# A four-layer conditioned network on one core: the layer-2 stencil with a turned result, row norms on ScalarE, and a planner with ranks by step

## The chip, the cores and the metric

The kernel runs on one core of a Trainium2 chip. The core has five engines with instruction queues of their own, each worked off in the order in which it was written: TensorE (PE; its weight loads are listed apart as PEld), VectorE (DVE), ScalarE (ACT), GpSimd (POOL) and SyncE (SP, which issues DMA transfers). They meet through semaphores. The metric is the device time of one launch in microseconds; the time before is 2741.08 us, the median of 3 runs (2740.74 to 2741.34).

## The reference, cut to what matters

Everything is fp32. A batch of 32 items, each a 256 x 256 matrix x (S tokens by D features), goes through four layers, one after the other:

```python
# layer 0: h from condB_t by two small linear layers; scale, shift = h @ Wsc + bsc, h @ Wsh + bsh
out = silu(scale * layer_norm(x) + shift) @ W_in + b_in        # norm over the whole 256x256 block
x = silu(scale * layer_norm(out) + shift) @ W_out + b_out + x
# layer 1: 16 heads of 16, 256 keys, a bias of 16x256x256 per item, padding mask
x = ln(x) * (1 + scale1) + shift1                               # norm over each row
x = x + softmax(q k^T / 4 + attention_bias, masked) v @ Wo
x = x + gelu_sigmoid(ln(x) * g2 + beta2 @ W1 + b1) @ W2 + b2
# layer 2: a finite-difference step on the 256x256 grid
Af, Bf = A_grid * f, B_grid * f
df = -(grad(Af[0], rows) + grad(Af[1], columns)) \
     + 0.5 * (grad2(Bf[0], rows) + grad2(Bf[1], columns) + mixed second derivative of Bf[2])
x = max(f + df * dt, 0)
# layer 3: causal attention with 16 heads and an exact-gelu feed-forward, gated by item
x = x + gate * (layer(x) - x)
```

`grad` and `grad2` are centred differences inside and one-sided ones in the first and last row or column. Along rows (partitions) they are a product with a banded 256 x 256 matrix.

## The kernel before, in words

A 256 x 256 matrix lies in SBUF as a tile [128, 2, 256]: row c*128 + p is on partition p. Weights stay in SBUF throughout. Each item runs through three generators, `layer_0`, `layer_1` (lines 931 and 956) and `layers_23` (line 1012), which record instructions and don't issue them.

The order is planned. `Order.record` notes each call with its engine, its dependencies, its length by a price list (`length`, line 145) and a rank, which is the value of `order.now` when it was recorded. The loop at lines 1087 to 1098 steps through all generators by time: item b's layer i starts at `b * PERIOD + START[i]`, and each `yield` moves its clock on by a nominal step times `PACE[i]`. `arrange` (line 186) then simulates the five engines and lets each take, of what is ready, the unit with the lowest rank; it counts PSUM banks (`CAPS`), a preference for staying in a tile shape on PE (`STAY`) and turns among the buffers of a tag. `emit` writes the instructions out in the order of their simulated starts. All instructions are therefore issued by line 327, and the profile has L327 for them; tiles tell them apart. So at one time PE works on layers of up to three items, in an order fixed when the kernel is built.

Steps that the text speaks of:

- The conditioning of layer 0 and layer 1 (lines 550 to 591), once: small matmuls with 128 x 128 weight blocks stationary and 32 items as moving columns; each block of the result gets its bias from one DVE instruction. Tiles `hidden`, `l0w`, `l0wss`, `w_ada`.
- `token_norm` (line 687): the norm of each row. DVE takes mean and variance, POOL the power -0.5 (`rstd`), and two DVE instructions write (x - mean) * rstd into tile `t`, which PE then turns (`mm<-ident,t`). Four calls an item: of x, of xm, of layer 2's x, of d.
- The stencil (lines 1024 to 1045). b2f, gd, a0f and b0f are products of f with grids; `gd` and `b0f` go through PE with the banded matrices `stencil` as stationary operand; `dd` (line 1052 on) is put together on DVE and added to the result. `small` holds products of edge columns.
- Attention: scores `sc` in four row groups of 32, bias subtracted by POOL (`nb`) and added by DVE with the running minimum (`pr`, `mn`), exponentials on ACT, transposes `tr` on PE, copied to `pt` by DVE and ACT in turns, and P·V in four column groups of 32.
- `add_row` and the differences on POOL write `x`, `xm`, `d`; all DMA transfers but a few at the start are issued by SP, in the planned order. Tile `x` has one buffer: the next item's load waits until this item's is read for the last time.

The lines of the stencil before:

```python
pm = mm_tile([P, C2, D])
for m in range(C2):
    with order.together():
        for i, u in enumerate((gd, b0)):
            for k in range(C2):
                pe.matmul(pm[:, m, :], lhsT=stencil[:, i, k, m * P : (m + 1) * P], rhs=u[:, k, :], ...)
```

Of the kernel before, what the change touches and what calls it, by code (L numbers as in the profile page):

```python
# [13 lines left out]
F32 = mybir.dt.float32  # L14
# [10 lines left out]
NFC = FF // P  # L25
HQ = 4
# [13 lines left out]
PERIOD = 90.3  # L40
START = (-51.7, 0.0, 118.1)
PACE = (1.27, 0.93, 1.0)
# [7 lines left out]
class Order:  # L50
# [8 lines left out]
    SETUP = 3e3  # L59
    HOP = 60.0  # L60
    TURN = 90.0
    SEEN = 165.0
    CAPS = {"sc": 5, "tr": 6, "mm": 8}
    EARLIER = {"sc": 12.4, "tr": -0.1, "mm": -2.0}
    STAY = 10.0
# [41 lines left out]
    def record(self, engine, call, method, args, kwargs):  # L107
# [11 lines left out]
        wide = [a for a in ins if math.prod(n for _, n in a.ap[1:]) >= 256]  # L119

        x["port"] = len(wide) > 1 and all(a.space != PSUM for a in ins + outs)
# [23 lines left out]
    def length(self, engine, method, outs, ins, args, kwargs):  # L145
# [5 lines left out]
        if engine == "pe":  # L151
# [5 lines left out]
            return max(free(outs[0]) / 1.2 + 2, 109.0) * passes, (rows, cols), slot  # L157
        if method == "dma_start":
            return sum(math.prod(k for _, k in a.ap) for a in outs) * 4
        if engine == "dve":  # L160
            if method == "reciprocal":
                return 120 + 8.3 * n, 40 + 8.3 * n
            if method == "tensor_tensor_reduce":
                return 240 + 1.05 * n, 150 + 1.05 * n
            if method == "tensor_scalar":
                a = (265 if columns else 150) + (1.06 if psum or not columns else 0.55) * n
            elif method == "scalar_tensor_tensor":
                a = 215 + 1.05 * n
            else:
                a = 148 + 1.05 * n  # L170
            return a, a - 80
# [8 lines left out]
        if method == "tensor_tensor":  # L180
            a = 600 if n <= 4 else 185 + 2.13 * n
        else:
            a = 185 + 0.86 * n
        return a, a - 40

    def arrange(self):
# [46 lines left out]
        dma = pool_end = 0.0  # L233
# [14 lines left out]
        while todo:  # L248
# [6 lines left out]
            for e in self.ENGINES:  # L255
                if free[e] > now:
                    continue
                while coming[e] and coming[e][0][0] <= now:
                    u = heapq.heappop(coming[e])[1]
                    heapq.heappush(ready[e][need[u]], (ranks[u], u))  # L260
                best = None
                for k, heap in ready[e].items():
                    if not heap or any(held[g] + m > room[g] for g, m in k):
                        continue
# [5 lines left out]
                    if best is None or rank < best[0]:  # L270
                        best = rank, k
# [8 lines left out]
                for x in units[u][2]:  # L280
                    if e == "pe":
# [4 lines left out]
                        elif its_shape != (P, P):  # L286
                            t = max(t, slots.get(slot, 0.0), pe_last + 6)
# [3 lines left out]
                        done = slots[slot] = t + one  # L291
                        pe_end = max(pe_end, done)
                        t = done if shape == (P, P) else t + 6
# [5 lines left out]
                    else:  # L299
                        x["start"] = now  # L300
                        more = 0.9 * max(pool_end - now, 0.0) if e == "dve" and x["port"] else 0.0
                        if e == "act" and x["length"][2] not in (None, table):
                            table, more = x["length"][2], self.TABLE
                        done, t = (now + a + more for a in x["length"][:2])
                        if e == "pool":
                            pool_end = done
                    end = max(end, done)
# [9 lines left out]
                for v in follow[u]:  # L317
                    may(v, now + 1)
                for v in after[u]:
                    may(v, now + 1 if units[v][0] == e and x["method"] != "dma_start" else end + self.HOP)  # L320

# [8 lines left out]
def _constants():  # L330
# [18 lines left out]
    stencil = np.stack([grad.T, grad2.T]).copy()  # L349
# [24 lines left out]
def kernel(ctx: ExitStack, tc: tile.TileContext, io, out, n_batch=B):  # L374
# [46 lines left out]
    scale_t = ctile("scale_t", [P, C2, B])  # L421
    shift_t = ctile("shift_t", [P, C2, B])
    ada_g = ctile("ada_g", [P, C2, B])
    ada_b = ctile("ada_b", [P, C2, B])
# [40 lines left out]
    def turned_vectors(tag, names, eng):  # L465
# [12 lines left out]
        return {name: cols[:, at] for name, at in vectors.items()}  # L478

    def load_x(b):  # L480
        x = sb.tile([P, C2, D], F32, tag="x", name="x", bufs=1)
# [7 lines left out]
    t_b = ctile("t_b", [P, B])  # L489
    sync.dma_start(t_b, io["condB_t"].partition_broadcast(P))  # L490
    vector = turned_vectors(
# [4 lines left out]
    i_b = ctile("i_b", [P, B], I32)  # L496
# [52 lines left out]


# [4 lines left out]
    pm = mm_tile([P, 4, B])  # L555
    for m in range(4):
        pe.matmul(pm[:, m, :], lhsT=w1[:, m * P : (m + 1) * P], rhs=enc, start=True, stop=True)
    for m in range(4):
# [575 lines left out]
```

## Time and profile before

| What | us |
| --- | --- |
| time, median of 3 runs | 2741.08 |
| profiled execution | 2742.87 |
| its span, first to last instruction | 2741.1 |
| PE busy | 2663.5 |
| DVE busy | 2327.2 |
| ACT busy | 1785.5 |
| POOL busy | 1537.2 |
| mean granted clock of PE, share of full | 0.993 |

The profile is of one execution. "Busy" is time in which at least one instruction of the engine ran. A line of groups reads: line, engine, operation, output<-inputs by tile names, shape and number, then busy us, mean ns of one, idle us ahead of them and who ended it. Matmuls are pipelined: an fp32 matmul shows as two instructions (passes) whose recorded durations overlap, so the pitch between starts tells what one costs. A line of stretches gives for each engine the busy time and (x number of instructions), then PE's granted clock, the busy share of DMA and its GB/s. A line of waits reads: who waited, for whom, total us, times, longest.

### The profile page before, as it was taken

The numbers are of one execution on the slowest core, as the hardware profiler recorded it, in microseconds if no ns is written. First come the engines' busy times: TensorE is split into PE (matmuls) and PEld (weight loads), VectorE is DVE, ScalarE is ACT, GpSimd is POOL, SyncE is SP. The second block draws the span as 40 slices with busy tenths as digits, with TensorE's granted clock in tenths as the row PEclk, the third lists the DMA queues.
The fourth block names the chain that finished last, engine by engine and source line by source line (L and its number), as shares of the span: only waits on it lengthen the run. The fifth ranks groups of instructions, "written<-read, shape, count | busy, mean of one in ns | idle before, by whom it ended". The sixth has DMA issues, their size and how long they took to land.

```text
span 2741.1 us, 59979 instructions
## 1 busy us (share of the span) xinstructions
PE 2663.5 (97%) x20330; PEld 2156.6 (79%) x20330; DVE 2327.2 (85%) x7665; ACT 1785.5 (65%) x5800; POOL 1537.2 (56%) x1896
## 2 busy tenths in 40 slices
PE   5899999999999999999999999999999999999997
PEld 5668888888888888888888888888888878888875
DVE  4689888889888888888888888888888888888873
ACT  1467676667677667667667667667667667667654
POOL 2556665556665556665556665556665556665430
PEclk9999999999999999999999999999999999999998
DMA  7222221112221112221112222112222112222100
GB/s 223 67 67 67 71 68 55 42 55 67 71 67 55 48 49 67 71 68 60 44 48 68 71 71 64 40 45 67 71 71 68 39 49 64 68 70 67 43 5 9
DMA packets 177446, 169.93 MB, mean 62 GB/s; under 512 B 19514, under 2 KB 175732, under 8 KB 177140
## 3 DMA queue, kind: packets, MB, share of 16 engines
q1 hardware_dynamic: 177104, 166.08, 19.7%
q8 instruction: 163, 2.67, 0.4%
q14 instruction: 143, 1.17, 0.1%
q10 hardware_dynamic: 36, 0.01, 0.0%
HBM read 157.66 MB, written 8.39 MB: 61 GB/s over the span
## 4 chain that ended last, share of the span: by engine, by line
PE 76%; POOL 13%; DVE 5%; DMA 2%; issue 2%; ACT 1%; SPq 0%; ACTq 0%; POOLq 0%; DVEq 0%
PE mm L327 60%; PE tr L327 10%; POOL nb L327 8%; PE sc L327 6%; POOL d L327 2%; DVE pr L327 1%; POOL rstd L327 1%; DVE st L327 1%; DVE d L327 1%; DMA nb<-in_fside_Bx16xSxS_dram 1%; POOL wide L327 1%; DVE t L327 1%; ACT pr L327 1%; DMA L1b<-in_L_cond_b_dram 0%; SPq L327 0%
## 5 line engine op out<-in xcount | busy, mean ns | idle before, releaser
L327 ACT ACTIVATE pr<-pr,mn 128x256 f32<-128x256 f32 (+1 forms) x2048 | 962.8, 477 | 218.7 <-DVE mn L327 214.2
L327 POOL TENSOR_TENSOR nb<-mask_f,nb 128x512 f32<-128x512 f32 x512 | 707.5, 1407 | 43.5 <-DMA nb<-in_fside_Bx16xSxS_dram 29.2
L327 PE MATMUL tr<-ident,pr 128*128 128x128 f32 x3584 | 507.4, 276 | 22.8 <-DVE mn L327 13.7
L327 PEld LDWEIGHTS tr<-ident,pr 128*128 128x128 f32 x3584 | 413.7, 141 | 119.2 <-ACT pr L327 50.3
L327 DVE CUSTOM_DVE_ANT_0 pr<-sc,nb 128x256 f32<-128x256 f32 x1024 | 379.7, 416 | 56.1 <-POOL nb L327 31.8
L327 ACT ACTIVATION_READ_ACCUMULATOR pr<-pr,mn 128x1 f32 x2048 | 396.7, 194 | 0.0
L327 DVE COPY pt<-tr 128x512 f32<-128x512 f32 (+1 forms) x512 | 308.4, 613 | 43.1 <-PE tr L327 42.8
L327 ACT COPY pt<-tr 128x512 f32<-128x512 f32 (+1 forms) x512 | 267.3, 528 | 104.5 <-PE tr L327 102.8
L327 DVE CUSTOM_DVE_ANT_0 pr<-sc,causal 128x128 f32<-128x128 f32 (+1 forms) x1024 | 296.1, 353 | 6.9 <-PE sc L327 6.8
L327 PE MATMUL sc<-k_t,nq 32*128 32x256 f32 (+1 forms) x4096 | 267.4, 374 | 0.0
L327 PE MATMUL mm<-h_t,L1w 128*128 128x256 f32 x1024 | 265.4, 390 | 0.6 <-DVE h_t L327 0.6
L327 PE MATMUL mm<-h_t,L3w 128*128 128x256 f32 x1024 | 247.0, 386 | 0.6 <-DVE h_t L327 0.6
L327 POOL TENSOR_SCALAR hid<-hid 128x256 f32<-128x256 f32 x256 | 124.9, 500 | 217.2 <-ACT hid L327 214.6
L327 PE MATMUL mm<-L3w,hid 128*128 128x256 f32 x1024 | 239.2, 382 | 4.3 <-ACT hid L327 4.3
L327 PE MATMUL mm<-L1w,hid 128*128 128x256 f32 x1024 | 240.0, 382 | 0.0
L327 PEld LDWEIGHTS mm<-L1w,hid 128*128 128x128 f32 x1024 | 187.1, 190 | 31.4 <-issue 9.9
L327 PEld LDWEIGHTS sc<-k_t,nq 32*128 32x128 f32 x4096 | 161.6, 184 | 62.8 <-issue 23.8
L327 PEld LDWEIGHTS mm<-L3w,hid 128*128 128x128 f32 x1024 | 189.3, 192 | 27.5 <-ACT hid L327 5.1
L327 PEld LDWEIGHTS mm<-h_t,L3w 128*128 128x128 f32 x1024 | 189.3, 192 | 27.0 <-DVE h_t L327 1.0
L327 ACT ACTIVATE k_t<-mm,cols 128x256 f32<-128x256 f32 x128 | 53.6, 470 | 233.0 <-PE mm L327 233.0
L327 PEld LDWEIGHTS mm<-h_t,L1w 128*128 128x128 f32 x1024 | 179.3, 192 | 26.8 <-DVE o L327 9.9
L327 POOL COPY wide<-rs 128x256 f32<-128x256 f32 x128 | 64.3, 502 | 192.4 <-DVE rs L327 179.7
(167 smaller groups left out, 4983.1 us busy)
## 6 DMA issues: line engine op xcount, KB each, us to landing
nb<-in_fside_Bx16xSxS_dram SPq DMA_DIRECT2D x512, 256.0 KB
x<-in_x_dram SPq DMA_DIRECT2D x32, 256.0 KB
out_dram<-d SPq DMA_DIRECT2D x32, 256.0 KB
mask<-in_mask_Bx1xSxS_bk_dram SPq DMA_DIRECT2D x32, 64.0 KB
L1w<-in_L_cond_W_dram SPq DMA_DIRECT2D x2, 1024.0 KB
L3w<-in_L_cond_W_dram SPq DMA_DIRECT2D x2, 1024.0 KB
l0w<-in_L_cond_W_dram SPq DMA_DIRECT2D x1, 1024.0 KB
g_b<-in_L_cond_B_grid_dram SPq DMA_DIRECT2D x3, 256.0 KB
```

The source lines that it names most:

```text
L327: call(*args, **kwargs)
```

## The change

Six things change together:

- The stencil multiplies the other way round. `gd` and `b0f`, in blocks of 128 x 128, are the stationary operand, and the stencil moves. Row block k only touches the 129 output rows next to it (`NEAR`), so each product has 129 columns. The two row blocks' results overlap in 2 columns (`BOTH`). The result comes out turned: ACT copies it into `rows_t`, DVE adds the overlap, and four PE transposes turn it back.
- `token_norm` computes `shift` = -mean * rstd on DVE and lets ACT write x * rstd + shift, two activations in place of two DVE instructions.
- The conditioning makes the 32 items the stationary operand, in four column tiles of 32, with the weights moving; the result is copied, turned by PE and given its biases in one DVE instruction.
- The two `small` products go from DVE to POOL.
- Tile x gets two buffers, mask one; `t_b` and `i_b` use buffers of attention tiles; the constant stencil is [128, 2, 2, 129] in place of [128, 2, 2, 256].
- The planner: new prices, a port that DVE and POOL share, PSUM banks shared between engines, small tiles on PE; new `CAPS`, `EARLIER`, `STAY`. Each generator is now recorded in one go, and its ranks are set by `PERIOD`, `START`, `PACE`, an offset for the first five and last five items (`EDGE`) and an offset for each step of a layer (`SHIFT`).

```diff
-PERIOD = 90.3
-START = (-51.7, 0.0, 118.1)
-PACE = (1.27, 0.93, 1.0)
+PERIOD = 86.0
+START = (-59.8, 0.0, 116.9)
+PACE = (1.37, 1.22, 1.08)
+EDGE = {(0, 0): -102.4, (0, 1): -3.5, (0, 2): 0.3, (1, 0): -29.2, ..., (31, 1): 3.6, (31, 2): -30.9}
+SHIFT = (
+    {0: -23.5, 1: -31.5, 2: -24.4, ...},
...
-    HOP = 60.0
-    TURN = 90.0
+    HOPS = {"act": 40.0, "dve": 40.0, "pool": 90.0, "pe": 60.0, "sync": 60.0}
+    OWNS = {"act": 30.0, "dve": 30.0, "pool": 83.0, "sync": 30.0}
+    TURN = 92.0
+    FIRST = {(32, P): 107.0, (P, 32): 27.0}
+    SLACK = 50.0
-    CAPS = {"sc": 5, "tr": 6, "mm": 8}
-    EARLIER = {"sc": 12.4, "tr": -0.1, "mm": -2.0}
-    STAY = 10.0
+    CAPS = {"sc": 6, "tr": 7, "mm": 6}
+    EARLIER = {"sc": 28.7, "mm": -1.9, "tr": 6.1}
+    STAY = 5.0
+    PORT = 0.05
...
-    stencil = np.stack([grad.T, grad2.T]).copy()
+    full = np.stack([grad.T, grad2.T], axis=1)
+    stencil = np.stack([full[:P, :, :NEAR], full[P:, :, S - NEAR :]], axis=2).copy()
...
-        x = sb.tile([P, C2, D], F32, tag="x", name="x", bufs=1)
+        x = sb.tile([P, C2, D], F32, tag="x", name="x")
...
+    def conditioning(dst, weights, src, bias):
+        pm = mm_tile([P, P])
+        with order.together():
+            for k in range(len(weights(0))):
+                for j in range(4):
+                    pe.matmul(
+                        pm[j * B : (j + 1) * B, :], lhsT=src[:, k, :], rhs=weights(j)[k],
+                        start=k == 0, stop=k == len(weights(0)) - 1,
+                    )
+        by_batch = sb.tile([P, P], F32, tag="h_t", name="by_batch")
+        dve.tensor_copy(by_batch, pm)
+        pm = mm_tile([P, 4, B])
+        pe.transpose(pm.rearrange("p j b -> p (j b)"), by_batch, ident)
+        dve.tensor_tensor(dst, pm, bias.unsqueeze(2).broadcast_to([P, 4, B]), ALU.add)
...
+        shift = sb.tile([P, C2], F32, tag="shift", name="shift", bufs=4)
+        dve.scalar_tensor_tensor(shift, mv[:, :, 0], -1.0, r, ALU.mult, ALU.mult)
         xn = sb.tile([P, C2, D], F32, tag=tag, name=tag, bufs=bufs)
         for c in range(C2):
-            dve.tensor_scalar(xn[:, c, :], x[:, c, :], mv[:, c, 0:1], r[:, c : c + 1], ALU.subtract, ALU.mult)
+            act.activation(xn[:, c, :], x[:, c, :], AF.Identity, bias=shift[:, c : c + 1], scale=r[:, c : c + 1])
...
-        mask = sb.tile([P, C2, S], U8, tag="mask", name="mask")
+        mask = sb.tile([P, C2, S], U8, tag="mask", name="mask", bufs=1)
...
-        dve.tensor_tensor(small, edges4(f), e_g, ALU.mult)
+        pool.tensor_tensor(small, edges4(f), e_g, ALU.mult)
...
-        pm = mm_tile([P, C2, D])
-        for m in range(C2):
-            with order.together():
-                for i, u in enumerate((gd, b0)):
-                    for k in range(C2):
+        halves = []
+        for k in range(C2):
+            pm = mm_tile([P, C2, NEAR])
+            halves.append(pm)
+            for d in range(C2):
+                with order.together():
+                    for i, u in enumerate((gd, b0)):
                         pe.matmul(
-                            pm[:, m, :], lhsT=stencil[:, i, k, m * P : (m + 1) * P], rhs=u[:, k, :],
-                            start=i == 0 and k == 0, stop=i == 1 and k == C2 - 1,
+                            pm[:, d, :], lhsT=u[:, k, d * P : (d + 1) * P], rhs=stencil[:, i, k, :],
+                            start=i == 0, stop=i == 1,
                         )
+        yield LAND
+        rows_t = sb.tile([P, C2, S], F32, tag="l2", name="rows_t", bufs=4)
+        act.copy(rows_t[:, :, 0:NEAR], halves[0])
+        act.copy(rows_t[:, :, NEAR:S], halves[1][:, :, BOTH:NEAR])
+        both = rows_t[:, :, NEAR - BOTH : NEAR]
+        dve.tensor_tensor(both, halves[1][:, :, 0:BOTH], both, ALU.add)
+        yield LAND
+        pm = transpose4(rows_t)
...
-    queue = []
     for b in range(n_batch):
         for i, layer in enumerate((layer_0, layer_1, layers_23)):
-            queue.append((b * PERIOD + START[i], len(queue), PACE[i], layer(b, res)))
...
+            trace(3 * b + i, layer(b, res), i, b * PERIOD + START[i] + EDGE.get((b, i), 0.0), PACE[i])
```

`trace` steps one generator to its end and sets `order.now` to its clock plus `SHIFT[layer]` of the step.

## The prediction

> **What bounds the kernel now.** I read the page first, then busy time by stretches of 86 us, then TensorE's (PE's) timeline of one batch, its waits, and last the rows of what is edited.
>
> ```profile
> PE 2663.5 (97%) x20330; PEld 2156.6 (79%) x20330; DVE 2327.2 (85%) x7665; ACT 1785.5 (65%) x5800; POOL 1537.2 (56%) x1896
> 0.00:86.00 86.00, 55.45 (x266) 44.43 (x270) 44.91 (x165) 20.49 (x62) 26.57 (x37) 0.94 0.64 199
> ...
> 1376.00:1462.00 86.00, 85.58 (x680) 69.25 (x682) 75.91 (x246) 59.25 (x189) 52.16 (x63) 1.00 0.21 63
> ...
> 2666.00:2741.00 75.00, 57.94 (x346) 43.09 (x344) 28.85 (x108) 33.82 (x99) 6.78 (x11) 0.89 0.02 8
> PE tr L327 <- DVE mn L327: 12.5, 29, 0.5
> ```
>
> The stretches list PE, its weight loads, DVE (VectorE), ACT (ScalarE), POOL (GpSimd), granted clock, DMA share and GB/s. Between 172 and 2600 us PE is busy 85.6 of every 86 us, and the last line is its only wait there: 0.43 us, once a batch. DVE, ACT and POOL have 10, 26 and 34 us to spare in a stretch. So in the middle a microsecond counts only if it is PE's. In the chain the piece "PE mm x78" stands at 243.45 and at 2535.40 us: 28 batches, (2535.40 - 243.45) / 28 = 81.86 us each. The rest, 2741.1 - 32 x 81.86 = 122 us, is filling and draining: PE idles 31 us in the first 86, some 13 in the next, and 21 after 2600.
>
> ```profile
> 1388.74 0.60 PE L327 MATMUL tr<-ident,pr 128*128 128x128 f32 x4
> 1389.18 0.60 PE L327 MATMUL mm<-ident,t 128*128 128x128 f32 x4
> ...
> 1406.84 0.28 PE L327 MATMUL mm<-mv,mean_mat 128*128 128x1 f32 x2
> 1406.98 1.11 PE L327 MATMUL mm<-h_t,L1w 128*128 128x256 f32 x4
> ...
> 1443.36 1.03 PE L327 MATMUL mm<-gd,stencil 128*128 128x256 f32 x4
> 1444.23 1.03 PE L327 MATMUL mm<-b0f,stencil 128*128 128x256 f32 x4
> 1445.09 0.60 PE L327 MATMUL mm<-ident,t 128*128 128x128 f32 x4
> ```
>
> Starts (first column) give the pitch; durations overlap. Four passes of 256 columns take 1445.09 - 1444.23 = 0.86 us, 0.216 each; four transposes of 128 columns 0.44, 0.110 each; two passes of one column 0.14, 0.070 each, each with a full 128x128 weight load.
>
> **The stencil.** An fp32 matmul is two passes. Before: 8 matmuls, 16 passes of 256 columns, 16 x 0.216 = 3.46 us. After: again 8 matmuls, with gd and b0 as weights and 129 columns of the stencil moving: 16 passes, then 4 transposes. No row shows 129 columns in two passes. The nearest row is the transpose (same weight size, 128 columns, 0.110); one more column by the slope to 256, (0.216 - 0.110) / 128, makes 0.111. So 16 x 0.111 + 4 x 0.110 = 2.21 us, and 1.25 us saved per batch. The other end is that a pass lasts as long as its weight load is recorded (stencil, 190 ns): 16 x 0.190 + 0.44 = 3.48 us, nothing saved. I take 0.111: the one-column row loads the same weights in two passes and has a pitch of 0.070, so the recorded load is latency. Batches 0 to 30 are under a full PE: 31 x 1.25 = 38.8 us.
>
> One rule speaks against this. The Trainium skill ("TensorE: Matmul & The Clock Gate", section "The mechanism") says a weight load overlaps a running matmul only where the row groups differ; with the same page's 128/1.2 = 107 ns per load ("LDWEIGHTS (loading the stationary operand)") a pass would be about 0.217 and the new stencil 3.9 us, an estimate that makes it slower than 3.46. The full-array transposes at 0.110 contradict it.
>
> ACT then copies the halves into rows_t (two COPYs; ctx_t's row has 363 ns, together 0.73), DVE adds the two overlapping columns (some 0.18, as the 176 ns of a 16-element product), and PE turns rows_t. This lies between PE's stencil and DVE's last use of the result; PE does other batches' work meanwhile. Its cover is that PE's written order has such work there; without it PE would wait 1.3 us a batch and the whole saving is gone. A second PSUM bank is held by it for some 1 us; I cost that at nothing, since no PE wait in the middle is for a bank.
>
> **Row norms.** Four per batch.
>
> ```profile
> L327 DVE TENSOR_SCALAR t<-x,mv,rstd 128x256 f32<-128x256 f32 x128 | 103.9, 852 | 5.1 <-POOL rstd L327 3.5
> L327 DVE TENSOR_SCALAR t<-d,mv,rstd 128x256 f32<-128x256 f32 x64 | 24.5, 425 | 6.9 <-POOL rstd L327 6.9
> L327 DVE TENSOR_SCALAR t<-xm,mv,rstd 128x256 f32<-128x256 f32 x64 | 23.6, 411 | 44.6 <-POOL rstd L327 44.6
> L327 ACT ACTIVATE h_t<-mm,ada_b,ada_g 128x256 f32<-128x256 f32 x64 | 32.6, 560 | 18.2 <-PE mm L327 18.2
> L327 DVE TENSOR_TENSOR small<-xm,e_dd 128x16 f32<-128x16 f32 x32 | 37.5, 1171 | 0.0
> ```
>
> DVE loses (103.9 + 24.5 + 23.6) / 32 = 4.75 us a batch and gains four two-element shifts (the dev rows, 215 to 273 ns): 0.9. ACT gains 8 x 0.56 = 4.5 us; a pair takes 1.02 us in the timeline. Each norm is later by the shift (0.25), the longer pair (1.02 for 0.73 undisturbed) and a hop: some 0.6 us, nothing while PE is full.
>
> The skill's "ScalarE: Activation LUTs", "Rules for kernel authors", would keep adds and multiplies on VectorE; by its section "What ACT_TABLE_LOAD costs" an ACTIVATE with two column operands is 186 + 186 + 213 = 585 ns, an estimate of 4.7 us a batch. The 560 ns row agrees on the price, and ACT is not the bound.
>
> **Moves to POOL.** The two `small` products leave DVE, (37.5 + 5.6) / 32 = 1.35 us; on POOL each costs between 0.26 (rs<-scale_t) and 0.70 (the power of rstd), up to 1.4 a batch, and queues before bias subtractions (1.41 each). Totals per batch: DVE 72.7 to about 68, ACT 55.8 to 61, POOL 48 to 49, PE 80.6. PE stays the limit. PE's one wait follows a chain of POOL d, POOL nb, DVE pr, ACT pr: DVE's relief shortens it, POOL's products lengthen it. Bounds: gone (29 x 0.43 = 12 us) or twice as long; I take half gone, 6 us, since DVE gives up three times what POOL gains.
>
> **Start.** The conditioning matmuls' 32 h2 and 32 scale/shift passes have PE from 14.96 to 31.3 us at 0.22 each, then scale_t and shift_t are there at 31.94. In column tiles four run side by side: the P·V product does that, 32 passes of 256 columns in 1.87 us. Of 128 columns, at half pace (256-column passes take 0.43 in this stretch), 32 passes take about 1.9. Each step gains a copy, a transpose and an add instead of four adds: +0.8. So 14.96 + 2 x (1.9 + 0.72 + 0.8) + 0.2 = 22.0, 9.9 us sooner. Batch 0's first layer hangs on it (its y starts at 36.09), but DMA is 95 to 99% busy from 24 to 48 us. Bounds 0 and 10; I take 8.
>
> **Order.** All priorities, batch offsets and planner prices are rewritten, x gets a second buffer (batch 1's load is issued at 62.54 us, when batch 0 has let go; now at once), mask loses one (its only reader is a 0.61 us cast, a batch ahead: nothing). On SP's queue x's load moves ahead of bias loads; the stencil's load halves. In the middle PE can't be fuller. From 60 to 172 us PE waits 20 us: bounds 15 gained, 5 lost; I take 4 gained, since batch 0's chain still leads. In the drain two norms lengthen the last chain by 1.2 us; the turned stencil there is 1.77 + 0.73 + 0.18 + 0.44 and hops, 3.5, as before. The last batch's rank moves, between 6 gained and 6 lost, taken as nothing.
>
> **Sum.** 38.8 + 6 + 8 + 4 - 1.2 = 55.6 us. The profiled execution has 2742.9 (span 2741.1 and 1.8 around it), 1.8 above the median 2741.08; from it the sum gives 2687.3, from the median 2685.5.
>
> **Rivals.**
> - More goes: PE's wait vanishes (12) and start, fill and drain give 10, 10 and 5: 2741.1 - 38.8 - 12 - 25 + 1.2 = 2666. For it: 122 us outside the middle; against: batch 0's chain has latencies that no order removes.
> - The stencil alone: start bound by DMA, the wait stays: 2741.1 - 38.8 + 1.2 = 2703. For it: the DMA share of 0.95 to 0.99.
> - The change doesn't shorten PE's work: passes at 0.190: 2741.1 - 12 + 1.2 = 2730. Against it, the 0.070 pitch.
> - Slower: norms queue on ACT, in order, behind exponentials, and PE's transposes of them wait. ACT is busy 9.4 and 9.9 of 10 us from 1450 to 1470. Two exponentials ahead cost about 1.0 us; 0.7 exposed for each of 31 x 4 norms is 87 us: 2741 - 56 + 87 = 2772. It decides from 56/124 = 0.45 us a norm. Against it: norms' transposes stand at 1404, 1429 and 1445, in stretches where ACT is busy 8.1, 7.5 and 7.3 of 10.
>
> **How the numbers follow.** Chances: forecast 0.57, more 0.14, stencil alone 0.13, no shorter PE 0.06, slower 0.10. The forecast's own range is 2668 to 2702. The whole one goes from 2655, all bounds of "more" near their ends, to 2722, short of the last two cases. A measurement tells 0.2% (5.5 us) from no change: faster 0.57 + 0.14 + 0.13 + 0.04 = 0.88, same 0.02, slower 0.10.
>
> **What would show it.** The period falls from 81.86 to about 80.5 us; stencil passes start 0.11 us apart; PE's waits in the middle stay under 0.5 us a batch; ACT's busy time rises by some 165 us and DVE's falls by as much; y of batch 0 starts near 27 us. Wrong if PE waits for t or for rows_t in the middle, if the passes' pitch is near 0.19, or if the rewritten order opens new waits each batch.

## The result and the profile after

The changed kernel takes 2710.07 us (median of 4 runs, 2707.02 to 2711.92), the kernel before 2741.21 beside it: a ratio of 0.9883, 95% interval 0.9866 to 0.9900. The forecast was 2685.5. The profiled execution of the changed kernel has 2711.45 us, its span 2709.7. Two lines of its page, span and busy time:

```profile
span 2709.7 us, 60241 instructions
...
PE 2616.1 (97%) x20462; PEld 2121.2 (78%) x20462; DVE 2166.8 (80%) x7499; ACT 1929.2 (71%) x6120; POOL 1570.6 (58%) x1960
```

DVE loses 160 us of work and ACT gains 144, as meant. PE loses 47. Two of the stretches that were shown for the kernel before (columns as in the prediction):

```profile
0.00:86.00 86.00, 48.51 (x352) 36.22 (x352) 54.57 (x196) 28.29 (x82) 36.89 (x54) 0.84 0.65 211
1376.00:1462.00 86.00, 84.96 (x677) 69.27 (x676) 72.03 (x256) 64.72 (x211) 49.21 (x61) 1.00 0.19 57
```

In the first stretch PE shows less busy time with 352 passes in place of 266; part of them are column tiles, which run side by side. In the middle PE is busy 84.96 of 86, less than the 85.58 before. The stencil itself came out as priced. PE's timeline of one batch:

```profile
1427.90 0.39 PE L365 MATMUL mm<-stencil,gd 128*128 128x129 f32 x2
1428.12 0.39 PE L365 MATMUL mm<-stencil,b0f 128*128 128x129 f32 x2
...
1429.46 0.39 PE L365 MATMUL mm<-stencil,b0f 128*128 128x129 f32 x2
1429.69 0.60 PE L365 MATMUL tr<-ident,pr 128*128 128x128 f32 x4
...
1432.73 0.60 PE L365 MATMUL mm<-ident,rows_t 128*128 128x128 f32 x4
1433.16 0.60 PE L365 MATMUL mm<-ident,x 128*128 128x128 f32 x4
```

Sixteen passes from 1427.90 to 1429.69, 0.112 us each, and 0.43 for the transposes: 2.22 us in place of 3.46, 1.24 saved. Yet the period from one batch's stencil to the next fell only from 81.86 to 81.31 us in the middle (81.29 to 81.33 for batches 11 to 21). PE's waits between 172 and 2560 us say why; the columns are total, times and longest:

```profile
PE mm L365 <- DVE ctx_t L365: 17.5, 17, 1.0
PE mm L365 <- ACT t L365: 3.6, 5, 0.9
```

PE's old wait (12.5 us for mn) is all but gone (0.8 us are left), and one of 1.03 us for ctx_t, the multiplied context of the attention, stands in its place. This is what precedes it in one batch, first on DVE, then on POOL:

```profile
1441.48 1.22 DVE L365 SCALAR_TENSOR_TENSOR shift<-mv,rstd 128x2 f32<-128x2 f32 x1 [0.41 <-POOL rstd L365]
1442.62 0.41 DVE L365 TENSOR_TENSOR ctx_t<-ctx_t,mm 128x256 f32<-128x256 f32 x1
```

```profile
1440.30 1.15 POOL L365 TENSOR_TENSOR rstd<-rstd,mhalf 128x2 f32<-128x2 f32 x1
1441.42 2.49 POOL L365 TENSOR_TENSOR nb<-mask_f,nb 128x512 f32<-128x512 f32 x2
```

The new shift, two elements on each partition, waits for rstd and then lasts 1.22 us, as long as the bias subtraction that POOL began 0.06 us earlier. The multiply that PE needs is queued behind it on DVE. The group of all 128 shifts has a mean of 429 ns, and the single ones fall in two groups. 37 began 0.06 to 0.6 us after a POOL instruction that reads two tiles (nb, x or a0f, 128x256 or 128x512) had begun; they took 0.68 to 1.22 us, and each ended some 0.02 us after that instruction. The other 91 took 0.14 to 0.16 us, among them two that began 13 ns ahead of a bias subtraction, and 31 beside POOL's power of rstd, which has two elements.

```profile
L365 DVE SCALAR_TENSOR_TENSOR shift<-mv,rstd 128x2 f32<-128x2 f32 x128 | 54.9, 429 | 50.4 <-POOL rstd L365 49.4
L365 ACT ACTIVATE t<-x,shift,rstd 128x256 f32<-128x256 f32 x128 | 70.0, 593 | 160.6 <-DVE shift L365 160.2
```

**Where the time went.** I priced every PE pass by the pitch of its shape in undisturbed stretches (0.216 us for 256 columns, 0.110 for 128, 0.070 for one; passes in row or column groups by the length of a whole block of them) and took the sum from the span. How the grouped passes are priced moves each difference by up to 1.6 us. What is left over is time that PE's work doesn't cover, by the stretch in which it arises:

| us of the span | before | after | difference |
| --- | --- | --- | --- |
| PE's work | 2561.4 | 2518.4 | -43.0 |
| not covered, to 172 us | 84.0 | 63.3 | -20.7 |
| not covered, 172 to 2494 us | 59.2 | 81.0 | +21.8 |
| not covered, 2494 us to the end | 36.5 | 47.0 | +10.5 |
| span | 2741.1 | 2709.7 | -31.4 |

So work and start gave 64 us, the middle took 22 back and the end 10. The experiments ask what the middle's loss is, and whether the parts of the change are worth what they were priced at.

### The profile page after: what moved, and what is told of

It is laid out like the page before. It is cut to its first block, busy times and chain, and to the rows that moved or that the text cites. A ratio compares the mean times of both kernels' runs of the same rounds, so it can differ in the third digit from the quotient of the medians.

```text
span 2709.7 us, 60241 instructions
## 1 busy us (share of the span) xinstructions
PE 2616.1 (97%) x20462; PEld 2121.2 (78%) x20462; DVE 2166.8 (80%) x7499; ACT 1929.2 (71%) x6120; POOL 1570.6 (58%) x1960
## 4 chain that ended last, share of the span: by engine, by line
PE 61%; POOL 25%; DVE 6%; issue 4%; ACT 2%; DMA 1%; SPq 0%; ACTq 0%; POOLq 0%; DVEq 0%
PE mm L365 45%; POOL nb L365 10%; PE tr L365 9%; PE sc L365 7%; POOL rstd L365 4%; POOL d L365 2%; POOL offset L365 2%; POOL mask_f L365 2%; DVE pr L365 1%; POOL cmf L365 1%; POOL b0f L365 1%; DVE st L365 1%; POOL a0f L365 1%; POOL cpf L365 1%; POOL small L365 1%
## 5 line engine op out<-in xcount | busy, mean ns | idle before, releaser
L365 POOL TENSOR_TENSOR nb<-mask_f,nb 128x512 f32<-128x512 f32 x512 | 683.9, 1355 | 60.7 <-DMA nb<-in_fside_Bx16xSxS_dram 46.6
L365 PE MATMUL tr<-ident,pr 128*128 128x128 f32 x3584 | 491.5, 275 | 8.1 <-ACT pr L365 2.5
L365 DVE CUSTOM_DVE_ANT_0 pr<-sc,nb 128x256 f32<-128x256 f32 x1024 | 387.7, 417 | 90.0 <-PE sc L365 87.0
L365 DVE CUSTOM_DVE_ANT_0 pr<-sc,causal 128x128 f32<-128x128 f32 (+1 forms) x1024 | 309.5, 350 | 57.9 <-PE sc L365 40.7
L365 POOL TENSOR_SCALAR hid<-hid 128x256 f32<-128x256 f32 x256 | 99.8, 405 | 373.1 <-ACT hid L365 372.9
L365 POOL COPY wide<-rs 128x256 f32<-128x256 f32 x128 | 53.5, 418 | 414.5 <-DVE rs L365 384.4
L365 PE MATMUL mm<-h_t,L1w 128*128 128x256 f32 x1024 | 252.2, 386 | 0.7 <-DVE mn L365 0.4
L365 PE MATMUL mm<-h_t,L3w 128*128 128x256 f32 x1024 | 249.5, 388 | 1.8 <-DVE h_t L365 1.3
L365 PEld LDWEIGHTS mm<-L1w,hid 128*128 128x128 f32 x1024 | 184.9, 190 | 21.8 <-issue 1.6
L365 ACT ACTIVATE t<-x,shift,rstd 128x256 f32<-128x256 f32 x128 | 70.0, 593 | 160.6 <-DVE shift L365 160.2
```

Source lines behind the costliest of these rows:

```text
L365: call(*args, **kwargs)
```

## The experiments

Times are medians; a ratio is to the kernel before on the same chip (2743 to 2746 us there). "The order held" means that the planner's result is kept and only the named instructions are replaced when the instructions are written out.

### The multiply ahead of the shift

The changed kernel, its order held, with 17 multiplies into ctx_t written out just ahead of the shift that stood before them.

```diff
     def emit(self):
         self.arrange()
         xs = [x for _, _, xs in self.units for x in xs]
+        ...
+        for x in on_dve:
+            if x["method"] == "tensor_tensor" and named(x, "ctx_t"):
+                ready = max(self.units[u][2][i]["start"] for u, i in x["deps"])
+                ahead = [s for s in shifts if max(x["start"] - 1600.0, ready + 300.0) < s < x["start"]]
+                x["start"] = min([x["start"]] + [s - 1.0 for s in ahead])
```

> The changed kernel with one thing moved: in 17 batches of the middle, DVE's multiply of ctx_t is written ahead of the shift of the row norm that stood just before it; all else keeps its order. Theory A: PE's wait of 1.03 us for ctx_t in these batches is the shift's doing (it waits for POOL's rstd and then for the port), so the wait goes in all 17 and the time falls by 13 to 18 us, to 2692 to 2697. Rival B: the multiply is late by itself (ACT's copy of ctx_t, or PE's transposes of wide), or the next wait takes its place: under 5 us gained, 2705 or more.

Measured: 2701.69 us (2699.41 to 2703.69), ratio 0.9844 (0.9830 to 0.9859); the changed kernel had 0.9883, so about 10.7 us less. The period is 80.92. PE's waits from 172 to 2560 us:

```profile
PE mm L373 <- ACT t L373: 15.6, 22, 0.9
PE mm L373 <- DVE mn L373: 0.8, 3, 0.4
```

The wait for ctx_t is gone, and PE now waits for t, the norm that the same shift feeds. So the shift's place in the queue was part of the loss. The 10.7 us lie between what theory A (13 to 18) and rival B (under 5) expected: the next wait took back a part. The shift's own length would explain it, since it holds up ctx_t when it stands ahead of it, and t in any case; the run with the shift on ACT tests that.

### POOL's power sooner as well

The same, with POOL's power of rstd written out straight behind the addition before it; in the changed kernel one bias subtraction of 1.27 us stands between them.

```diff
+        begun = {}
+        for engine, _, (x, *_) in self.units:
+            for t in x["tiles"]:
+                if engine == "pool" and t.source_name == "rstd":
+                    if x["method"] == "tensor_scalar":
+                        begun[t.name] = x["start"]
+                    elif t.name in begun:
+                        x["start"] = begun.pop(t.name) + 1.0
```

> The changed kernel with the 17 multiplies of ctx_t moved ahead of the shift, as before, and on POOL each power of rstd written straight behind its addition, ahead of the bias subtractions that stood between. With the multiplies alone PE still waited 0.7 us a batch, then for the norm's tile t, behind rstd, shift and two activations. Theory A: that wait is the norm's chain, which gets up to 1.3 us shorter: it goes, and the time falls by another 8 to 15 us. Rival B: another wait takes its place, or the bias subtractions come late: within 4 us of the run with the multiplies alone, or slower.

Measured: 2707.38 us, ratio 0.9867 (0.9852 to 0.9882), some 6 us slower than the multiply's move alone; period 81.2. PE's waits:

```profile
PE mm L381 <- DVE dev L381: 12.0, 17, 0.7
PE mm L381 <- DVE h_t L381: 5.1, 4, 1.6
PE mm L381 <- ACT t L381: 0.9, 1, 0.9
```

The wait for t went from 15.6 to 0.9 us, and waits for DVE's dev and h_t of another layer took its place: this is rival B. Bringing rstd forward moves the delay to another chain through the same two engines. At 1437.85 us DVE's instruction into x (128x512) is held for 1.82 us beside three bias subtractions that POOL began at 1437.86, and dev comes behind it at 1439.59.

### The shift on ACT

The changed kernel, its order held, with the shift taken off DVE: ACT turns the mean's sign while POOL's power runs and makes each of the two shifts with one activation of one element. The computation is the same.

```diff
-            call, args, kwargs = x["call"]
-            call(*args, **kwargs)
+            if x["method"] == "scalar_tensor_tensor" and any(t.source_name == "shift" for t in x["tiles"]):
+                shift, mean, _, r = args[:4]
+                begun = max(self.units[u][2][i]["start"] for u, i in x["deps"] if self.units[u][0] == "pool")
+                calls.append((begun, n, (self.act.activation, (mean, mean, AF.Copy), {"scale": -1.0})))
+                for c in range(C2):
+                    calls.append((x["start"] + c, n, (
+                        self.act.activation, (shift[:, c : c + 1], mean[:, c : c + 1], AF.Identity), {"scale": r[:, c : c + 1]},
+                    )))
+            else:
+                calls.append((x["start"], n, x["call"]))
```

> The changed kernel with its planned order held; shift is not computed by DVE's two-element instruction but by ACT: one two-element copy that turns the mean's sign while POOL's power runs, and two one-element activations with scale rstd (encodings' rows of 128x32 take 0.23 us, so some 0.25 each) ahead of the norm's two. Theory A, the wait in the middle comes from the shift, which lasts 1.22 us while POOL's bias subtraction runs and stands ahead of the ctx_t multiply on DVE: the ctx_t wait (17 times 1.03 us) goes, t comes some 0.5 us sooner than in the changed kernel, so the wait for t that replaced it when the multiply was put first (0.7 us) goes too; period 80.2 to 80.7 in the middle and 2688 to 2700 us. Rival B, the next wait takes its place: ACT, 2 us a batch busier, hands on the delay through exponentials or t, period 80.9 or more, 2700 to 2712 us. Rival C: the wait for ctx_t stays, so it does not come from the shift.

Measured: 2681.17 us (2679.69 to 2685.53), ratio 0.9777 (0.9762 to 0.9791). That is 29 us under the changed kernel and 7 under the best that theory A allowed. The period is 80.16 to 80.25 us from batch 11 to 20, as theory A expected (80.2 to 80.7). PE has no wait for ctx_t on DVE left; its longest between 172 and 2560 us:

```profile
PE mm L377 <- ACT hid L377: 2.2, 3, 1.9
PE mm L377 <- ACT t L377: 1.5, 4, 0.5
```

The next run has the same order on PE up to 1978 us, and its profile stands for both below.

### Other ranks at the end

The same, and other values in EDGE for the first layers of the last items.

```diff
-(27, 0): 7.3, (27, 1): 1.5, ... (28, 2): 4.6, (29, 0): 2.1, ...
+(26, 0): 12.1, (26, 2): 1.2, (27, 0): 3.0, (27, 1): 0.0, ... (28, 2): 5.4, (29, 0): 4.8, ...
```

> The changed kernel with shift on ACT, as in the run before (2681.17 us), and other rank offsets for the first layers of items 26 to 29 (six values of EDGE, moved by 0.8 to 12 us). Theory A, the drain's loss is set by when the last five items start: the middle is as in the run with shift on ACT (no wait for ctx_t, period 80.2 to 80.7), the order changes only after about 2200 us, and the end comes 1 to 6 us sooner, 2675 to 2680 us. Rival B, the loss lies in the last item's own chain (from its first norm of layer 2 to the last row), which these offsets do not touch: 2680 to 2684 us, no difference that the measurement tells.

Measured: 2683.00 us (2680.14 to 2685.93), ratio 0.9772 (0.9756 to 0.9789): no different from the run before. These offsets, moved by 0.8 to 12 us, are not what sets the drain; rival B's own place for the loss, the last item's chain, was not tested apart. The profile, with a span of 2682.6 us, shows what the shift on ACT does. PE's longest waits from 172 to 2560 us:

```profile
PE mm L377 <- ACT t L377: 2.4, 6, 0.7
PE mm L377 <- ACT hid L377: 2.3, 3, 1.9
```

The 17.5 us of waits for DVE's ctx_t are gone, the period is 80.21 to 80.29 us from batch 11 to 20, and 59.1 us of the stretch from 172 to 2494 us are not covered by PE's work, 81.0 in the changed kernel. The norm in one batch, on ACT and then on POOL:

```profile
1426.62 0.48 ACT L377 ACTIVATE shift<-mv,rstd 128x1 f32<-128x1 f32 x2 [2.79 <-POOL rstd L377]
1427.01 1.08 ACT L377 ACTIVATE t<-x,shift,rstd 128x256 f32<-128x256 f32 x2
```

```profile
1426.56 2.68 POOL L377 TENSOR_TENSOR nb<-mask_f,nb 128x512 f32<-128x512 f32 x2
```

The same bias subtraction starts just ahead of the shift, and the shift is now done in 0.48 us: t starts 0.39 us after the shift does, where it had to wait 1.22 on DVE. So the changed kernel's loss in the middle is the DVE shift. With it gone the period is 1.07 us shorter, about the one wait for ctx_t. Of the 27.1 us by which the span is shorter, some 22 arise between 172 and 2494 us, 2 before and 3 behind.

### All changed instructions in the order of before

The changed instructions with the planner, ranks and prices of before (PERIOD 90.3, START, PACE, no EDGE or SHIFT, the old CAPS and lengths).

```diff
-PERIOD = 86.0
-START = (-59.8, 0.0, 116.9)
-PACE = (1.37, 1.22, 1.08)
-EDGE = {(0, 0): -102.4, ...}
-SHIFT = (...)
+PERIOD = 90.3
+START = (-51.7, 0.0, 118.1)
+PACE = (1.27, 0.93, 1.0)
...
-    CAPS = {"sc": 6, "tr": 7, "mm": 6}
+    CAPS = {"sc": 5, "tr": 6, "mm": 8}
```

> The changed instructions (turned stencil, norms on ScalarE, column tiles, two x buffers, small on POOL) under the planner of before: its prices, ranks and stepping. Theory A: what was lost in the middle (0.7 us a batch) and in the drain (11 us) belongs to the new order, not to the instructions; with the old order the turned stencil's 1.24 us a batch arrives whole (31 x 1.24 = 38) and some 8 of the start: 2741 - 46 = 2695, between 2685 and 2703. Rival B: the norms on ScalarE and the longer chain of an item cost this under any order: 2708 or more.

Measured: 3024.78 us, ratio 1.1015 (1.0997 to 1.1032), period 90.45 to 92.1. PE's two longest waits and the line of the stretch, both 400 to 2400 us:

```profile
PE mm L329 <- POOL wide L329: 49.5, 22, 2.3
PE tr L329 <- ACT pr L329: 44.4, 44, 1.7
400.00:2400.00 2000.00, 1884.12 (x13880) 1479.26 (x13880) 1464.67 (x5077) 1316.74 (x4178) 1057.11 (x1340) 0.95 0.18 53
```

Theory A falls. Less work in an order found for other work is 10% slower. Not all of that is waiting: the granted clock is 0.95 of full in this stretch, where the kernel before has 1.00. By an estimate from this, 0.05 x 2000 us, up to 100 of the 280 us can lie in the lower clock; why it fell was not tested. The ranks are tuned to the instruction set, so this run says nothing on the price of the parts.

### The turned stencil alone, planned anew

The kernel before with the turned stencil alone, and its planner run with before's ranks.

```diff
-        pm = mm_tile([P, C2, D])
-        for m in range(C2):
...
+        halves = []
+        for k in range(C2):
+            pm = mm_tile([P, C2, NEAR])
+            halves.append(pm)
+            for d in range(C2):
+                with order.together():
+                    for i, u in enumerate((gd, b0)):
+                        pe.matmul(pm[:, d, :], lhsT=u[:, k, d * P : (d + 1) * P], rhs=stencil[:, i, k, :], ...)
+        yield LAND
+        rows_t = sb.tile([P, C2, S], F32, tag="l2", name="rows_t", bufs=4)
...
+        pm = transpose4(rows_t)
```

> The kernel before with the turned stencil alone. Theory A: PE's work falls by 1.24 us a batch and all of it arrives, as PE is full in the middle: 2741 - 38 = 2703, within 2698 and 2708. Rival B: the two ACT copies, the DVE add and the later transposes make PE wait in the middle, and half or less of it arrives: 2720 or more.

Measured: 3004.48 us, ratio 1.0946 (1.0930 to 1.0963), period 90.1 to 90.8, with waits for hid (65.9 us) and t (29.5) from 400 to 2400 us, and a granted clock of 0.95 there as well. Theory A falls here too, and the lesson is the same: one step more in layer 2 and the ranks no longer fit. Such a run doesn't price the part; the runs of the stencil and of the norms further down hold the order.

### The changed instructions with norms on DVE, old planner

```diff
-        shift = sb.tile([P, C2], F32, tag="shift", name="shift", bufs=4)
-        dve.scalar_tensor_tensor(shift, mv[:, :, 0], -1.0, r, ALU.mult, ALU.mult)
...
-            act.activation(xn[:, c, :], x[:, c, :], AF.Identity, bias=shift[:, c : c + 1], scale=r[:, c : c + 1])
+            dve.tensor_scalar(xn[:, c, :], x[:, c, :], mv[:, c, 0:1], r[:, c : c + 1], ALU.subtract, ALU.mult)
```

> The changed instructions with the row norms left on DVE, under the planner of before. Beside the run with the norms on ScalarE under the same planner: theory A says that the norms' place is worth less than 6 us either way under an order in which PE is full; rival B says that the norms on ScalarE cost 0.7 us a batch, so that this one is faster than that one by 15 us or more.

Measured: 3005.00 us, ratio 1.0954 (1.0936 to 1.0972), waits for h_t (58.6 us) and pr (37.7) from 400 to 2400 us, granted clock 0.97. It is 20 us faster than the same with norms on ACT, as rival B expected (15 or more), but both are far from any order that fits, so the 20 us are no price either. The new planner with norms on DVE wasn't tried.

### The turned stencil in the old slots

Before's order held; the 16 stencil passes take the old ones' places, copies and transposes follow at fixed delays. The coupling of rows 127 and 128 is left out; the number of passes is the same, of 128 columns each.

```diff
+            for x, (d, (i, u)) in zip(group, [(d, iu) for d in range(C2) for iu in enumerate((gd, b0))]):
+                x["instead"] = [(0.0, (nc.tensor.matmul, (pm[:, d, m * P : (m + 1) * P],), dict(
+                    lhsT=u[:, m, d * P : (d + 1) * P], rhs=stencil[:, i, m, m : m + P], start=i == 0, stop=i == 1,
+                )))]
+        group[-1]["instead"] += [
+            (600.0, (nc.scalar.copy, (rows_t[:, :, 0:P], pm[:, :, 0:P]), {})),
+            ...
```

> The kernel before, planned as before and written out in its order, with the turned stencil put into the places of the old one: 128-column matmuls in the slots of the old ones, then two ACT copies, a small DVE instruction and four PE transposes 0.6 to 4 us of planned time later. It leaves out the coupling of rows 127 and 128 (so that one PSUM bank does) and keeps the number and size of the instructions. The run with the same edit and a new plan was 260 us slower. Theory A: that was the order that the old ranks give for another set of instructions; in the order of before the stencil's 1.24 us a batch arrives: 34 to 42 us less than the kernel before. Rival B: the turned stencil itself stalls the engines (copies, hops): 19 us less or fewer, or slower.

Measured: 2740.13 us (10 runs), ratio 0.9985 (0.9975 to 0.9995): 4 to 5 us where 38 were priced. PE's work is 40 us less by the pitches, and the period is 81.85, as before. The time went into waits and stretched passes between 1444 and 1457 us: behind the stencil's first half PE waits 0.34 us for mn, and a block of 16 score passes takes 1.82 us where it took 1.15 before. The chain that ended last, there, of the kernel before:

```profile
1452.35 0.75 DVE dd L327
1453.44 0.34 DVE pr L327
1453.85 0.37 SPq L327
1454.26 2.02 DMA nb<-in_fside_Bx16xSxS_dram
1456.31 0.43 DVE pr L327
1456.74 0.34 DVE pr L327
1457.23 0.63 PE tr L327 x4
```

And with the turned stencil in its slots, first the score passes, then the chain:

```profile
1448.82 1.82 PE L332 MATMUL sc<-k_t,nq 32*128 32x256 f32 x16
```

```profile
...
1453.67 0.37 SPq L332
1454.08 2.03 DMA nb<-in_fside_Bx16xSxS_dram
...
1457.06 0.63 PE tr L332 x4
```

Before, the chain leaves PE at 1441.03 and comes back at 1457.23, through POOL, DVE's d, dd and pr, SP's queue and a load of nb. With the turned stencil it touches PE from 1445.20 to 1450.3 and then takes the same way: PE's return at 1457 moved by 0.17 us. These are rival B's numbers, but the turned stencil's own steps (rows_t) are not in the chain in this stretch. PE's work got shorter and the way around it didn't. So a PE that is busy 99.5% of the time had a second limit just behind it.

### Less DVE work in that stretch, without and with the stencil

Two runs with before's order held, in which DVE's product b1f and its subtraction are not computed.

```diff
         b1 = prod(g_b1, "b1f", dve)
+        order.units[-1][2][0]["instead"] = []
...
         dve.tensor_tensor(dd[:, :, 1:n], dd[:, :, 1:n], b1[:, :, 1:n], ALU.subtract)
+        order.units[-1][2][0]["instead"] = []
```

> The kernel before with its order held and one thing left out: DVE's product b1f and its subtraction from dd, which are not computed at all (2.77 us of DVE a batch, between 1438 and 1461 us in batch 17's stretch). PE's work is not touched. Theory A, DVE is a second limit just behind PE in that stretch: PE's one wait there (0.43 us for mn) shrinks or goes, the period falls by at most 0.45 us, from 81.86 to between 81.4 and 81.7, and the time by 5 to 14 us, because PE is then the only limit. Rival B, only PE counts there: the same, 0 to 14 us less. This run alone does not tell them apart; it is the reference for the next.

Measured: 2735.65 us (7 runs), ratio 0.9971 (0.9960 to 0.9982): 8 us less, inside what both theories allow. The second run puts the turned stencil in its slots as well:

> The run with the turned stencil in the old order's slots, and b1f and its subtraction left out as well (neither is computed; the coupling of rows 127 and 128 is left out too, as in the first run of the stencil in place). Theory A, DVE had swallowed the stencil's saving: with 2.8 us of DVE a batch gone the saving of 1.24 us a batch shows in full, the period falls to 80.6 or less, and the time is 30 to 42 us under that of the run without b1f alone. Rival B, the turned stencil's own copies and transposes bring waits: the time is, as it was with b1f in, some 5 us under the run without b1f (0 to 12).

Measured: 2723.68 us, ratio 0.9928 (0.9911 to 0.9944): 12 us under the run without b1f, at the top of rival B's bounds and far from theory A's 30 to 42. Relieving DVE raised what the stencil brings from 5 to 12 us, no more. In this run's chain SP's queue and the load of nb no longer stand in that stretch. It leaves PE at 1430.19 and comes back at 1434.57, between the two halves of the stencil, by way of the row norm of d: DVE's difference and statistics, POOL's power, DVE's t, then pr and mn. Four pieces of it, and PE's wait at its end:

```profile
1430.21 0.70 DVE d L332
1432.27 0.70 POOL rstd L332
1433.33 0.41 DVE t L332
1433.74 0.33 DVE pr L332
```

```profile
1434.57 0.63 PE L332 MATMUL tr<-ident,pr 128*128 128x128 f32 x4 [0.34 <-DVE mn L332]
```

PE has 9.8 us of such waits for mn between 172 and 2560 us, 29 times, and the run without the stencil 0.2. By the pitches, some 0.7 of the 1.24 us a batch are lost in the 2 us behind the stencil's first half, as in the run with b1f. So the second limit has more than one way around PE: without b1f the one through the load of nb no longer shows, and the row norm of d, through DVE and POOL, still takes more than half of the saving. No run relieved that one.

### The norms on ACT in the old slots

Before's order held; the shift on DVE at the place of the first old norm instruction, the activations 0.3 us behind.

```diff
+            order.units[-1][2][0]["instead"] = [
+                (0.0, (nc.vector.scalar_tensor_tensor, (shift, mv[:, :, 0], -1.0, r, ALU.mult, ALU.mult), {}))
+            ][: 1 - c] + [
+                (300.0, (nc.scalar.activation, (xn[:, c, :], x[:, c, :], AF.Identity), dict(bias=shift[:, c : c + 1], scale=r[:, c : c + 1])))
+            ]
```

> The kernel before in its own order, with the four row norms changed in place: in the slot of DVE's two instructions stand the shift on DVE and two activations on ACT. Theory A: under an order in which PE is full and the norms have slack it is hidden: within 6 us of the kernel before. Rival B: each norm comes later by the shift, by its wait for the port and by the longer pair, and an order that was written for the short one makes PE wait for it: 0.5 us or more for some of the four, 15 to 60 us slower.

Measured: 2780.72 us, ratio 1.0132 (1.0116 to 1.0147): 36 us slower, period 82.97. A piece of its chain:

```profile
1444.05 1.45 ACT pr L330 x7
1445.50 0.98 ACT t L330 x2
1446.48 0.50 ACT pr L330 x2
...
1447.03 0.44 PE tr L330 x2
```

The norm's two activations stand between exponentials, and PE's transposes of pr wait for the exponentials behind them. This is the "slower" rival's mechanism, seen from the other side: it's the exponentials that queue behind norms. But the chain also passes a long shift on DVE, once in a period:

```profile
1404.30 1.23 DVE shift L330
1405.55 1.09 ACT t L330 x2
```

The two shares of the 36 us were not separated. Together they are 36 / 124 = 0.29 us a norm here, under the 0.45 from which the rival would have decided alone.

### The conditioning alone

The kernel before with the conditioning in column tiles, planned anew; here before's ranks do fit.

```diff
+    def conditioning(dst, weights, src, bias):
+        pm = mm_tile([P, P])
...
+    conditioning(h2, lambda j: [w2[:, k, part(j)] for k in range(4)], h1s, vector["L0_cond_b2"])
```

> The kernel before with the conditioning in column tiles alone, planned as before (the order on PE changes at the start only). Theory A: batch 0's first layer starts sooner by some 9 us and the fill keeps 6 to 11 us of it. Rival B: DMA or the rest of the fill takes it back: less than 4 us.

Measured: 2737.59 us (10 runs), ratio 0.9974 (0.9965 to 0.9983): 7 us less. Batch 0's first product of layer 0 starts at 32.39 us in place of 40.73. PE's work falls by 2.8 us, the time not covered up to 172 us from 84.0 to 79.2.

## Why the prediction was right and wrong

**The price of the stencil: right.** 1.24 us a batch by the pitches against 1.25; the passes stand 0.112 us apart against 0.111. The bound that nothing is saved (0.190) fell, and so did the rule on weight loads that spoke against the change.

**"So in the middle a microsecond counts only if it is PE's": the step that failed.** It was read from PE's busy time and PE's own waits. Held against the old order, the priced 38 us gave 5, since the chain there runs for 16 us through DVE, SP and a load. In the changed kernel the same sentence let the norms' delay cost "nothing while PE is full"; the shift in it cost 29 us, some 22 of them in the middle. The chain of waits, a view of the same page, had the other limit in it.

**PE's one wait: wrong.** "I take half gone, 6 us." The old wait did go, as in the bound "gone", but a new one came: the time not covered in the middle rose by 21.8 us where 6 were to go. The term that was mis-sized is the shift, "0.25" by the dev rows. It is 0.16 us alone and up to 1.22 beside POOL. The dev rows were the wrong neighbours: dev goes through DVE's tensor_scalar with one tile moving and single columns beside it, and never took over 0.28 us; the shift reads two tiles. The right neighbour stood in the prediction's own list, `small<-xm,e_dd` with a mean of 1171 ns for 16 elements. In the kernel before it comes in a pair with one of the same shape:

```profile
L327 DVE TENSOR_TENSOR small<-xm,e_g x32: 174/176/177, 128.4 to 2654.7; 128x16 f32<-128x16 f32 x32
L327 DVE TENSOR_TENSOR small<-xm,e_dd x32: 1156/1160/1269, 128.5 to 2654.8; 128x16 f32<-128x16 f32 x32
```

The three times are the shortest, the median and the longest in ns. All 32 of the first began some 0.05 us before POOL's a0f, which reads two tiles; all 32 of the second began 0.04 to 0.14 us after it, and ended with it. The Trainium skill ("SBUF — State Buffer", section "Who interferes with whom") says that a DVE instruction with two SBUF inputs contends with a GpSimd instruction that reads SBUF, that the port pair they share is an exclusive lock, and that issue order decides who blocks. The trace agrees, for a mere two elements: the shift begins 0.06 us after the 1.27 us subtraction and ends with it, and all 37 long shifts began second. It doesn't hold beside every POOL instruction: the power of rstd reads SBUF too, and the 31 shifts that began beside it took 0.15 to 0.16 us. The planner doesn't see the two-element case either, since its port counts only operands of 16 elements or more.

**Start and fill: undersized.** "8" for the conditioning against 7 measured by itself. "4" for the order and x's second buffer, bounded at 15, where the time not covered by 172 us fell by 20.7 in all, 4.8 of that with the conditioning alone. The difference, about 16, is just above that bound; order and buffer were not tested apart. x of batch 1 is first used at 30.17 us in place of 73.05, and PE has batch 1 to fill batch 0's gaps. "y of batch 0 starts near 27 us" took the wrong row. The y at 36.09 is `y<-mm,mean,gamma_t`, which doesn't need scale and shift, and it now starts at 19.8; the one that does need them, `y<-y,rs,offset`, starts at 26.1 in place of 38.4.

**Drain: undersized.** "-1.2" against -10.5. The last item's chain from its first stencil pass to the end is about as long as before (80.4 us against 80.0). But less of it is covered by PE's work: some 34 us aren't, 28.5 before, and in the stretch from 2494 us to that stencil some 5 more than before. Part of this is not waiting but slower passes. These are the stretches from 2494 us to the end, before and after, with the granted clock third from the end:

```profile
2494.00:2741.10 247.10, 225.50 (x1648) 178.32 (x1646) 171.74 (x572) 143.29 (x457) 94.63 (x116) 0.97 0.11 33
2494.00:2709.70 215.70, 190.11 (x1331) 149.58 (x1322) 125.02 (x442) 122.44 (x387) 63.48 (x87) 0.92 0.06 18
```

In the changed kernel 16 passes of `mm<-h_t,L1w` at 2599.74 us take 3.62 us, and 16 of the same shape, `mm<-h_t,L3w` at 2623.09, take 6.39. By an estimate from the records, passes at the lower clock cost 5 us over their pitch before and 12 after, some 6 of the 10.5 us. Why the clock is lower was not tested. An item now spends 232 us between its first projection in layer 1 and its last product, 197 before, and its x is first used 330 us ahead of that product, 246 before. That this deeper overlap is why less is left at the end is argued, not tested; other end ranks didn't change it.

**The rivals.** In microseconds the result is nearest to "the stencil alone" (2703), but not by its mechanism: the start did get shorter, 7 us of it by the conditioning alone, and the wait that PE has is another one. The tell-tale that came true is "the rewritten order opens new waits each batch": the one for ctx_t came 17 times in some 29 batches. The forecast's own range, 2668 to 2702, lies below the result; the whole one, up to 2722, holds it, and that is partly luck. The stencil brought what was forecast, but middle and end together are 37 us worse than the terms say (6 and -1.2 forecast, -21.8 and -10.5 measured), and some 12 us more at the start than forecast hid a part of that. With the shift on ACT the kernel takes 2681.17 us and the period is 80.2, where the prediction had 2685.5 and 80.5: the forecast's size was there to be had with that one instruction moved, though not by the same terms.

## What to carry to other kernels

A busy engine is not the only limit: follow the chain of waits through a period, and where it leaves that engine for some 16 us, a saving on it is worth little until the chain is shorter as well. Price a small instruction by what runs beside it and by how many tiles it reads, not by its size; a two-element step on DVE can take as long as the 512-element POOL instruction beside it, and a few small operations on ACT, which kept their length here, may beat it. And price the parts of a change with the order held: an order found for one set of instructions may not fit another.

## What the runs showed of the hardware

- A DVE instruction of two elements on each partition with two SBUF operands takes 0.14 to 0.16 us alone and up to 1.22 us beside a POOL tensor operation of two tiles (128x512, 1.27 us) that began ahead of it; this sorts all 128 shifts of the changed kernel, 91 short and 37 long. On ACT the one-element instructions that replaced it take 0.277 to 0.322 us in all 256 cases, whatever POOL does.
- fp32 passes of 129 columns, each with a 128x128 weight load of its own, follow each other every 0.112 us, though the load alone is recorded with 0.19.
- A POOL product of 128x16 elements (small) takes 0.22 to 0.67 us, median 0.40. On DVE before, the one that began just after POOL's a0f took 1.16 (median), the other, of the same shape, 0.176.
